# Layer 1's feed-forward blocks in the seven-product form, and the token sums on GpSimd

## The chip, the core and the metric

The kernel runs on one core of a Trainium2 chip. Five engines work side by side, each through its own instructions in order: TensorE (PE, matrix products), VectorE (DVE), ScalarE (ACT), GpSimd (POOL, which also issues the indirect DMAs) and SyncE (SP, which issues plain DMAs). They wait for one another through semaphores. The metric is the device time of one execution in microseconds (us); lower is better.

## The reference

Two layers of a graph transformer over 2708 tokens of width 512, f32, eight heads, each token attending to itself and its neighbours in `adj` (five to a few dozen):

```python
q = (h @ Wq.T + bq); k = (h @ Wk.T + bk); v = (h @ Wv.T + bv)
scores = einsum('nhd,mhd->hnm', q, k) / sqrt(64)     # -1e9 where mask == 0
ctx = einsum('hnm,mhd->nhd', softmax(scores), v)
h1 = layer_norm(h + ctx @ Wo.T + bo)
ff = relu(h1 @ W1.T + b1) @ W2.T + b2                # W1: 2048 x 512
h2 = layer_norm(h1 + ff)
```

## The kernel before

The kernel (`by_edges`) sorts the tokens by their number of neighbours into 22 tiles of 128 (the last has 20) and works on eleven **blocks** of two tiles. The order of all five engines is written out by hand: what stands first in the code stands first in its engine's queue.

The attention runs on DVE, ACT and POOL alone. For each tile, POOL gathers the rows of keys and values of its neighbours (L1113, one gather for one neighbour of 128 tokens; two gathers make a **chunk**). DVE multiplies keys by q (L1150), sums over a head's 64 columns (L1156), ACT makes the exponentials and scales half of the values (L1169, L1176), DVE scales the other half (L1182) and adds up (L1189). `advance(x)` in the block loop puts about x chunks of this into the queues; the tables `PACE` and `PACE7` say how much at which f. `until(g)` puts all that tile g still needs.

PE does the dense work. One block's feed-forward is a loop over 16 slices f of the 2048 hidden columns: four products of 256 columns into `pf` (L1523, or L1653 in the other form), ACT's relu into `ft`, and then the second product with W2. In the **plain form** (`feed_forward`) this is one 512-column product for each f and tile, into `a0` and `a1` (L1496). In the **seven-product form** (`feed_forward_by_seven`) two slices f and the two halves of W2's columns are taken together as a 2 x 2 product of 128 x 128 and 128 x 256 parts, and by sums of the parts (Strassen's, in Winograd's form) seven 256-column products replace eight. It needs for each of the seven pairs j four **token sums** of 128 x 128 (`sums`, L1625 to L1628, on DVE), three **weight sums** t2, t3, t4 and one changed quarter of W2 (`form`, L1592 to L1595), and at the block's end eight adds out of four PSUM places (a0, a1, c0, c1; L1695 to L1703) instead of two (L1567). The eighth pair is done plainly. The sums of pair j-1 are issued at f = 2j, the products of pair j-2 after the odd f (`products`). The three slots for t2, t3, t4 are reloaded from DRAM for every pair (`ask_forms`, L1610).

Layer 0 has the plain form in blocks 0, 1 and 10 and the seven-product form in blocks 2 to 9; the weight sums are made in block 1. All of layer 1 has the plain form. In layer 0, each block also has the K and V products of the block before (`keys_values`, L1732 to L1740). In the middle of each block the next block's o product is made (L620 from `attended`), added to the residual (L1455) and normalised; the norm's reciprocal root is one POOL instruction (L1275), between two DVE instructions (L1276, L1281). At a layer-1 block's end the two tiles zA and zB are normalised and scattered to the output by POOL (L1076). The queries of layer 1 are made before its first block, except those of tiles 21 and 0, which are made in block 0 (`asking`).

Of the kernel before, what the change touches and what calls it, by code (L numbers as in the profile page):

```python
# [483 lines left out]
def by_edges(ctx: ExitStack, tc: tile.TileContext, x, xT, adj, layers, out, redo):  # L484
# [71 lines left out]
    form_d = dram.tile([NFC // 2 - 1, 3, P, 2 * P], F32, name="form_d")  # L556
# [745 lines left out]
    class Layer:  # L1302
# [284 lines left out]
        def form(self, j):  # L1587
# [3 lines left out]
            t2, t3, t4 = self.slots if j < NFC // 2 - 2 else self.other_slots  # L1591
# [4 lines left out]
            for i, t in enumerate((t2, t3, t4)):  # L1596
                nc.sync.dma_start(out=form_d[j, i], in_=t)
# [7 lines left out]
        def ask_forms(self, upto):  # L1605

            while self.asked < upto:
                n = self.asked
                j, i = n // 3 % (NFC // 2 - 1), (2, 0, 1)[n % 3]
                nc.sync.dma_start(out=self.slots[i], in_=form_d[j, i])  # L1610
                self.asked += 1

        def feed_forward_by_seven(self, k, block, hs, hT):
# [6 lines left out]
            base = 3 * J * (k - FORMED - 1)  # L1620

            def sums(j):
                f0, f1 = fts[2 * j], fts[2 * j + 1]
                s = self.sums[j % 2]
                nc.vector.tensor_tensor(s[:, 0], f1[:, P:], f0[:, P:], ALU.add)  # L1625
                nc.vector.tensor_tensor(f0[:, P:], f0[:, :P], f0[:, P:], ALU.subtract)
                nc.vector.tensor_tensor(s[:, 1], s[:, 0], f0[:, :P], ALU.subtract)
                nc.vector.tensor_tensor(s[:, 2], f1[:, :P], s[:, 1], ALU.subtract)  # L1628
# [251 lines left out]
    for n in range(NL):  # L1880
        last = n == NL - 1
        nxt = None if last else Layer(n + 1, layers[n + 1])
        if n > 0:
# [37 lines left out]
            asking = now.queries(blocks[AHEAD])  # L1921
            next(asking)
            finish(streamed)
            now.apart = False
            now.load_w2(NFC // 2 - 1)
        hs, hT = early[n]
        projecting = xbs = None
        for k, block in enumerate(blocks):
            more = k + 1 < NB
            if k or n == 0:  # L1930
                asking = iter(())
            if n > 0 and 0 < k < NB - AHEAD:
                asking = now.queries(blocks[k + AHEAD])
# [9 lines left out]
            for f, zs in enumerate(working):  # L1943
# [16 lines left out]
                if more and f == NFC - 1:  # L1960
                    finish(asking)
# [120 lines left out]
```

## Time and profile before

| | us |
|---|---|
| median of three runs (1830.05 to 1832.14) | 1830.28 |
| span of the profiled execution | 1827.1 |
| layer 0, blocks 2 to 9, each | about 76.3 |
| layer 1, blocks 1 to 8, each | about 63.7 |

The profiled execution's own time is its span; the runs' times lie about 3 us above it. In the profile a row of a group names the line, the engine, the operation, what it writes and reads, the count, then the busy time, the mean of one in ns, and the idle time of the engine before it with what ended it. A row in order of time starts with the start and the length in us.

### The profile page before, as it was taken

What the parts mean: (1) busy time and instruction counts of PE and PEld (TensorE: products, weight loads), DVE (VectorE), ACT (ScalarE), POOL (GpSimd) and SP (SyncE); (2) the same over time, 40 slices, a digit from 0 to 9 for tenths busy, and PEclk for the clock granted to TensorE, in tenths of its full rate; (3) what the DMA queues carried; (4) which work ended last, traced back from release to release, by engine and by line L of the source; (5) the groups of instructions that cost most, each with busy time, mean ns of one, the idle gap of its engine ahead of it and who ended that gap; (6) DMA issues with size and microseconds to landing.
All of it is one profiled execution on the core that took longest, in us unless ns stands there. A gap on an engine that the chain in (4) does not pass through costs nothing.

```text
span 1827.1 us, 22528 instructions
## 1 busy us (share of the span) xinstructions
PE 1807.5 (99%) x6563; PEld 1162.6 (64%) x6563; DVE 1457.5 (80%) x2447; ACT 949.1 (52%) x3271; POOL 798.9 (44%) x745
## 2 busy tenths in 40 slices
PE   9999999999999999999999999999999999999998
PEld 4444456666777867778677644666666666666666
DVE  5887778988989889898895257887898888889853
ACT  5771435645556545564543213665665565567531
POOL 3334755534455544454430042353464555456302
PEclk9999999999999999999999999999999999999999
DMA  9997987757576676765652876745564664555300
GB/s 340 369 335 256 371 283 245 236 169 241 195 255 228 197 236 196 219 233 181 228 191 70 287 257 248 285 160 180 178 228 150 228 224 169 195 197 194 133 14 21
DMA packets 158061, 393.80 MB, mean 216 GB/s; under 512 B 17514, under 2 KB 60894, under 8 KB 157928
## 3 DMA queue, kind: packets, MB, share of 16 engines
q0 software_dynamic: 70608, 252.12, 40.2%
q1 hardware_dynamic: 77162, 118.55, 18.7%
q10 hardware_dynamic: 10158, 21.61, 3.1%
q8 instruction: 53, 0.87, 0.2%
q14 instruction: 80, 0.66, 0.1%
HBM read 338.78 MB, written 53.44 MB: 215 GB/s over the span
## 4 chain that ended last, share of the span: by engine, by line
PE 89%; DVE 5%; issue 2%; ACT 2%; DMA 1%; POOL 1%; POOLq 0%; SPq 0%; DVEq 0%
PE pf L1523 18%; PE a L1496 17%; PE pf L1653 9%; PE k L620 8%; PE v L620 8%; PE q L620 8%; PE o L620 8%; PE c L1643 4%; PE a L1643 3%; PE tp L1293 2%; DVE sc L1156 1%; DVE kv L1150 1%; DMA forms<-form_d 1%; PE a L1677 1%; PE a L1673 1%
## 5 line engine op out<-in xcount | busy, mean ns | idle before, releaser
L1113 POOL DMA_INDIRECT kv<-kv_d,listed x420 | 524.0, 1248 | 291.2 <-DVE acc L1189 133.9
L1523 PE MATMUL pf<-hT,w 128*128 128x256 f32 (+1 forms) x1792 | 393.2, 367 | 0.1
L1523 PEld LDWEIGHTS pf<-hT,w 128*128 128x128 f32 x1792 | 323.5, 190 | 103.1 <-issue 64.4
L1496 PE MATMUL a<-w,ft 128*128 128x512 f32 x800 | 373.1, 592 | 0.0
L1176 ACT ACTIVATE kv<-kv,p 128x64 f32<-128x64 f32 x1232 | 311.0, 335 | 5.0
L1275 POOL TENSOR_TENSOR rd<-va,mhalf 128x1 f32<-128x1 f32 (+1 forms) x88 | 80.5, 914 | 520.6 <-DVE va L1273 520.5
L1150 DVE TENSOR_TENSOR kv<-kv,q 128x1024 f32<-128x1024 f32 (+1 forms) x222 | 256.9, 1157 | 13.3 <-DMA q<-q_d,ident_i 10.9
L1156 DVE TENSOR_REDUCE sc<-kv 128x16 f32<-128x1024 f32 (+1 forms) x222 | 257.9, 1162 | 7.6
L1189 DVE TENSOR_TENSOR acc<-acc,kv 128x1024 f32<-128x1024 f32 (+2 forms) x178 | 205.4, 1154 | 37.6 <-ACT kv L1176 23.0
L1653 PE MATMUL pf<-hT,w 128*128 128x256 f32 x1024 | 233.1, 379 | 1.6 <-ACT ft L1664 1.6
L1496 PEld LDWEIGHTS a<-w,ft 128*128 128x128 f32 x800 | 150.1, 190 | 113.2 <-issue 101.3
L1653 PEld LDWEIGHTS pf<-hT,w 128*128 128x128 f32 x1024 | 193.9, 190 | 35.4 <-issue 7.9
L1534 ACT ACTIVATE ft<-pf,b 128x256 f32<-128x256 f32 (+1 forms) x208 | 95.0, 459 | 197.6 <-PE pf L1523 195.2
L1169 ACT ACTIVATE p<-sc,listed 128x8 f32<-128x8 f32 x420 | 104.0, 296 | 147.2 <-DVE sc L1156 135.7
L620 PE MATMUL o<-wo,cT 128*128 128x512 f32 x336 | 151.0, 593 | 1.0 <-ACT cT L1298 1.0
L1664 ACT ACTIVATE ft<-pf,b 128x256 f32<-128x256 f32 x96 | 44.9, 468 | 160.5 <-PE pf L1653 160.5
L1182 DVE TENSOR_TENSOR kv<-kv,p 128x512 f32<-128x512 f32 (+1 forms) x178 | 123.4, 693 | 4.5 <-ACT p L1169 4.3
L620 PEld LDWEIGHTS o<-wo,cT 128*128 128x128 f32 x336 | 63.4, 190 | 74.7 <-issue 65.5
L745 DVE MAX8 tops<-code 128x8 f32<-128x247 f32 (+2 forms) x242 | 78.6, 400 | 28.3 <-ACT code L740 28.3
L1281 DVE SCALAR_TENSOR_TENSOR h<-h,rd,ln_b 128x512 f32<-128x512 f32 (+1 forms) x88 | 65.9, 749 | 39.5 <-POOL rd L1275 39.5
L1220 ACT ACTIVATE cx<-acc,su 128x64 f32<-128x64 f32 (+1 forms) x352 | 88.2, 333 | 12.9 <-DVE su L1212 7.4
L1455 DVE TENSOR_TENSOR h<-o,xb 128x512 f32<-128x512 f32 (+1 forms) x44 | 30.3, 688 | 80.0 <-PE o L620 65.0
(232 smaller groups left out, 2323.5 us busy)
## 6 DMA issues: line engine op xcount, KB each, us to landing
aj<-in_adj SPq DMA_DIRECT2D x42, 677.0 KB, 6.3
forms<-form_d SPq DMA_DIRECT2D x168, 128.0 KB, 4.2
kv_d<-kvs ACTq DMA_DIRECT2D x21, 512.0 KB, 5.5
xg<-in_xT SPq DMA_DIRECT2D x19, 512.0 KB, 7.4
w<-in_W SPq DMA_DIRECT2D x16, 512.0 KB, 6.2
kv<-kv_d,listed POOLq DMA_INDIRECT x420, 6.3
zT_d<-zT SPq DMA_DIRECT2D x22, 256.0 KB, 5.1
xb_d<-h SPq DMA_DIRECT2D x21, 256.0 KB, 5.7
```

The source lines that it names most:

```text
L620: nc.tensor.matmul(o[:r], xs(c), wm[:, c, :], start=(c == 0), stop=(c == NC - 1))
L1113: return nc.gpsimd.indirect_dma_start(out=to, out_offset=None, in_=table[:, :], in_offset=bass.IndirectOffsetOnAxis(ap=s, axis=0), bounds_ ...
L1150: nc.vector.tensor_tensor(kv[:r, :c, :DM], kv[:r, :c, :DM], self.q[:r].unsqueeze(1).to_broadcast([r, c, DM]), ALU.mult,)
L1156: nc.vector.tensor_reduce(self.sc[:r, s0 : s0 + c, :], kv[:r, :c, :DM].rearrange("p s (h d) -> p s h d", d=DK), AX.X, ALU.add,)
L1169: nc.scalar.activation(p[:r, s, :], self.sc[:r, s, :], AF.Exp, bias=minus[:r, g, s : s + 1])
L1176: nc.scalar.activation(to[:, i, hd], kv[:r, i, DM + h * DK : DM + (h + 1) * DK], AF.Copy, scale=p[:r, s0 + i, h : h + 1],)
L1182: nc.vector.tensor_tensor(to[:, 0, :].rearrange("p (h d) -> p h d", d=DK), kv[:r, 0, DM:].rearrange("p (h d) -> p h d", d=DK), p[:r, s0, : ...
L1189: nc.vector.tensor_tensor(self.acc[:r, :c, :], self.acc[:r, :c, :], kv[:r, :c, DM:], ALU.add)
L1496: nc.tensor.matmul(a[:r, cols], fts[f][:, c0 : c0 + r], self.w2[f // 2][:, f % 2, cols], start=(f == 0), stop=(f == NFC - 1),)
L1523: nc.tensor.matmul(pf[:, :w], self.w1[f // 2][:, c, f % 2 * P : f % 2 * P + P], hT[:, c, :w], start=(c == 0), stop=(c == NC - 1),)
L1643: nc.tensor.matmul(to, left, right, start=start, stop=stop)
L1653: nc.tensor.matmul(pf[:, :W], self.w1[j][:, c, f % 2 * P : f % 2 * P + P], hT[:, c, :], start=(c == 0), stop=(c == NC - 1),)
```

## The change

Layer 1's blocks 0 to 9 take the seven-product form (`FIRST7`), with a pace table of their own. The weight sums of layer 1 are made in layer 0's last block, at f = 7, 9, ... 15 and after the first two queries, into places of the gathers' buffers (`staged`), and stored to a DRAM tile for each layer. All queries of layer 1 come before its first block, so that the place of Wq is free for the slots. The four token sums go from DVE to POOL, in both layers. The pools of `pf` and of the other products have two PSUM places each in layer 1, as in layer 0's blocks of that form, instead of three. The scatters of zA and zB stand behind each tile's norm.

```diff
-PACE7 = (0.0,) * 4 + (0.6,) + (1.3,) * 4 + (0.6,) * 2 + (0.0,) * 2 + (0.5, 0.8, 2.4)
+PACE7 = (
+    (0.0,) * 4 + (0.6,) + (1.3,) * 4 + (0.6,) * 2 + (0.0,) * 2 + (0.5, 0.8, 2.4),
+    (0.0,) * 3 + (0.7, 0.7, 1.2, 0.7, 1.2, 0.7, 1.2, 0.6, 0.0, 0.0, 1.0, 0.7, 1.9),
+)
 FORMED = 1
+FIRST7 = (FORMED + 1, 0)
...
-    form_d = dram.tile([NFC // 2 - 1, 3, P, 2 * P], F32, name="form_d")
+    form_d = [dram.tile([NFC // 2 - 1, 3, P, 2 * P], F32, name=f"form_d{n}") for n in range(NL)]
...
-        def form(self, j):
+        def staged(self):
+            slots = []
+            for _ in range(3):
+                place = at.tile([P, SLOTS, 2 * DM], F32, tag="kv", name="forms", bufs=KVB)
+                place = place.rearrange("p s n -> p (s n)")
+                slots += [place[:, i * 2 * P : (i + 1) * 2 * P] for i in range(8)]
+            return [slots[3 * j : 3 * j + 3] for j in range(NFC // 2 - 1)]
+
+        def form(self, j, slots=None):
...
-            t2, t3, t4 = self.slots if j < NFC // 2 - 2 else self.other_slots
+            t2, t3, t4 = slots or (self.slots if j < NFC // 2 - 2 else self.other_slots)
...
-                nc.vector.tensor_tensor(s[:, 0], f1[:, P:], f0[:, P:], ALU.add)
-                nc.vector.tensor_tensor(f0[:, P:], f0[:, :P], f0[:, P:], ALU.subtract)
-                nc.vector.tensor_tensor(s[:, 1], s[:, 0], f0[:, :P], ALU.subtract)
-                nc.vector.tensor_tensor(s[:, 2], f1[:, :P], s[:, 1], ALU.subtract)
+                nc.gpsimd.tensor_tensor(s[:, 0], f1[:, P:], f0[:, P:], ALU.add)
+                nc.gpsimd.tensor_tensor(f0[:, P:], f0[:, :P], f0[:, P:], ALU.subtract)
+                nc.gpsimd.tensor_tensor(s[:, 1], s[:, 0], f0[:, :P], ALU.subtract)
+                nc.gpsimd.tensor_tensor(s[:, 2], f1[:, :P], s[:, 1], ALU.subtract)
...
             norm(zA, P, self.g2, self.e2, between=lambda: stB.append(spread(zB)))
+            if self.n == NL - 1:
+                put(out, ident_i[:, block[0] : block[0] + 1], zA, "out")
             norm(zB, P, self.g2, self.e2, stB[0])
+            if self.n == NL - 1:
+                put(out, ident_i[:, block[1] : block[1] + 1], zB, "out")
...
-            streamed = now.queries(order[18 : 2 * AHEAD])
+            streamed = now.queries(order[18:])
             next(streamed)
             now.query(order[17], both[:, 1])
-            advance(0.6)
-            next(streamed)
-            advance(0.6)
+            for _ in order[18:21]:
+                advance(0.6)
+                next(streamed)
...
             now.load_w2(NFC // 2 - 1)
+            now.prepared()
...
-            seven = n == 0 and FORMED < k < NB - 1
+            seven = FIRST7[n] <= k < NB - 1
...
-            if n == 0 and k in (FORMED + 1, NB - 1):
+            if k in (FIRST7[n], NB - 1):
                 places_of_psum(3 - seven, seven)
...
                         nxt.load_second(0, temp)
+                        staged = nxt.staged()
+                    if f > 6 and f % 2:
+                        nxt.form((f - 7) // 2, staged[(f - 7) // 2])
...
                 nxt.query(*pool.pop(0))
+                nxt.form(6 - len(pool) % 2, staged[6 - len(pool) % 2])
```

The line numbers of the new program differ by 4 to 17. POOL's queue in a layer-1 block before, from one block's end to the next o (rd is the reciprocal root, out the scatter to the output, kv a gather):

```order
L1275 TENSOR_TENSOR rd<-va,mhalf 128x1
L1076 DMA out<-h,ident_i 2708x512
L1275 TENSOR_TENSOR rd<-va,mhalf 128x1
L1076 DMA out<-h,ident_i 2708x512
L1113 DMA kv<-kv_d_112,listed 128x1024 x14
L1275 TENSOR_TENSOR rd<-va,mhalf 128x1 x2
```

The same place in the new program, up to the third of the block's seven groups of token sums (`forms` and `ft` are the places of the sums and of the relu's results):

```order
L1279 TENSOR_TENSOR rd<-va,mhalf 128x1
L1080 DMA out<-h,ident_i 2708x512
L1279 TENSOR_TENSOR rd<-va,mhalf 128x1
L1080 DMA out<-h,ident_i 2708x512
L1638 TENSOR_TENSOR forms<-ft 128x128
L1639 TENSOR_TENSOR ft<-ft 128x128
L1640 TENSOR_TENSOR forms<-forms,ft 128x128
L1641 TENSOR_TENSOR forms<-ft,forms 128x128
L1117 DMA kv<-kv_d_112,listed 128x1024 x2
...
L1117 DMA kv<-kv_d_112,listed 128x1024 x4
L1638 TENSOR_TENSOR forms<-forms 128x128
```

Five groups of four sums now stand between the second scatter and the root of the next o, among the gathers; a sixth stands between the two roots and a seventh behind them.

DVE's queue at the end of a layer-1 block before (h is first the block's input with the residual, then the output; a is PSUM):

```order
L1567 TENSOR_TENSOR h<-a_10928,h 128x512
L1269 BN_STATS st<-h 128x6
L1271 BN_AGGR mv<-st 128x2
L1273 TENSOR_SCALAR va<-mv 128x1
L1276 SCALAR_TENSOR_TENSOR h<-h,mv,ln_g 128x512
L1281 SCALAR_TENSOR_TENSOR h<-h,rd,ln_b 128x512
L1150 TENSOR_TENSOR kv<-kv,q 128x2x512
```

The same place in the new program (u are the partial results of the two sums that both tiles share):

```order
L1193 TENSOR_TENSOR acc<-acc,kv 128x1024
L1709 TENSOR_TENSOR h<-u_10752,h 128x256
L1710 TENSOR_TENSOR u_10752<-c_10197,u_10752 128x256
L1711 TENSOR_TENSOR u_10753<-c_10198,u_10752 128x512
L1712 TENSOR_TENSOR h<-c_10198,h 128x256
L1713 TENSOR_TENSOR h<-a_10195,h 128x512
L1714 TENSOR_TENSOR h<-a_10196,h 128x512
L1715 TENSOR_TENSOR h<-u_10753,h 128x256
L1716 TENSOR_TENSOR h<-h,u_10753 128x512
L1273 BN_STATS st<-h 128x6
```

Eight adds stand where each tile had one, ahead of both norms.

More of the change, by code (lines that the diff above doesn't have):

```diff
@@ L1596, in form @@
             for i, t in enumerate((t2, t3, t4)):
-                nc.sync.dma_start(out=form_d[j, i], in_=t)
+                nc.sync.dma_start(out=form_d[self.n][j, i], in_=t)
         def form_back(self, j):
@@ L1609, in ask_forms @@
                 j, i = n // 3 % (NFC // 2 - 1), (2, 0, 1)[n % 3]
-                nc.sync.dma_start(out=self.slots[i], in_=form_d[j, i])
+                nc.sync.dma_start(out=self.slots[i], in_=form_d[self.n][j, i])
                 self.asked += 1
@@ L1619, in feed_forward_by_seven @@
             fts = []
[L1620 removed]
+            base = 3 * J * (k - FIRST7[self.n])
             def sums(j):
@@ L1929, in by_edges @@
             more = k + 1 < NB
[L1930 to L1933, printed above, removed]
-            seven = n == 0 and FORMED < k < NB - 1
+            seven = FIRST7[n] <= k < NB - 1
             if n == 0 and k == FORMED:
                 now.prepared()
-            if n == 0 and k in (FORMED + 1, NB - 1):
+            if k in (FIRST7[n], NB - 1):
                 places_of_psum(3 - seven, seven)
@@ L1960, in by_edges @@
                 if more and f == NFC - 1:
-                    finish(asking)
                     hT = now.turned(blocks[k + 1], hs_next)
-                advance((PACE7 if seven else (PACE if k else PACES)[n])[f])
-                if f in (0, 3, 7, 9) and (f or k):
-                    next(asking, None)
+                advance((PACE7[n] if seven else (PACE if k else PACES)[n])[f])
                 if k == 0 and len(now.w1) < NFC // 2 and f % 2 == 0:
```

2 lines of the change are left out of this document (removed).

## The prediction

> **What bounds the kernel now.** I read the page first, then the chain in order of time, then the windows block by block, then who waits for whom on VectorE (DVE) and GpSimd (POOL).
>
> ```profile
> span 1827.1 us, 22528 instructions
> PE 1807.5 (99%) x6563; PEld 1162.6 (64%) x6563; DVE 1457.5 (80%) x2447; ACT 949.1 (52%) x3271; POOL 798.9 (44%) x745
> ```
>
> TensorE (PE) has work in 99% of the span. That is the bound of the average; the change acts on one kind of stage, the layer-1 blocks, so I read the bound there.
>
> ```profile
> 1398.27 5.15 PE a L1496 x12
> 1403.42 6.91 PE pf L1523 x32
> ```
>
> A 512-column matmul instruction takes 5.15/12 = 0.429 us of PE, a 256-column one 6.91/32 = 0.216 us, back to back. Both forms run at the same rate per column.
>
> ```profile
> 1334.50:1398.30 63.80, 63.80 (x226) 41.21 (x225) 59.21 (x80) 37.67 (x142) 33.38 (x28) 1.00 0.59 212
> ...
> sum 382.30, PE 382.30 PEld 246.78 DVE 337.49 ACT 237.22 POOL 194.65; mean PE 63.72 PEld 41.13 DVE 56.25 ACT 39.54 POOL 32.44
> DVE h L1455 <- PE o L620: 22.3, 9, 3.6
> DVE h L1281 <- POOL rd L1275: 12.0, 24, 1.6
> ```
>
> The columns of a window are its length, then PE, weight loads, DVE, ACT, POOL, the granted clock and the DMA share. Six layer-1 blocks in a row take 63.7 us each; PE has no gap, DVE works 56.25 us of each. DVE's idle time is 382.3 - 337.5 = 44.8 us in six blocks. Of this, 22.3 us is waiting for PE's o product, 3.7 us a block. That is all the slack DVE has; the other 22.5 us (3.75 a block) are waits on POOL and ACT that stay. So PE bounds these blocks, with DVE 3.7 us behind it.
>
> **What PE gives up.** A pair of f has four 512-column products, eight instructions, 8 x 0.429 = 3.43 us; in the new form seven 256-column products, 14 x 0.216 = 3.02 us. That is 0.41 us a pair, 2.9 a block of seven pairs, 28.6 us over ten blocks: a PE floor of 63.7 - 2.9 = 60.8 us. It is real only where nothing else is later than 60.8.
>
> **What DVE gets.** The end of a layer-1 block has two adds now; in the new form it has the eight adds that layer 0's blocks already show.
>
> ```profile
> L1567 DVE TENSOR_TENSOR h<-a,h 128x512 f32<-128x512 f32 x12 | 7.9, 661 | 0.0
> 621.72 0.37 ACT L1695 COPY u<-c 128x256 f32<-128x256 f32 x1 [0.62 <-PE c L1643]
> 622.81 10.52 PE L1653 MATMUL pf<-hT,w 128*128 128x256 f32 x48
> 624.12 0.37 DVE L1696 TENSOR_TENSOR h<-u,h 128x256 f32<-128x256 f32 x1
> 628.20 0.68 DVE L1269 BATCH_NORM_STATS2 st<-h 128x6 f32<-128x512 f32 x1
> 631.62 0.93 POOL L1275 TENSOR_TENSOR rd<-va,mhalf 128x1 f32<-128x1 f32 x1 [1.25 <-DVE va L1273]
> 633.78 0.28 DVE L1627 TENSOR_TENSOR forms<-forms,ft 128x128 f32<-128x128 f32 x1
> 634.48 0.59 PE L1643 MATMUL c<-forms 128*128 128x256 f32 x2
> ```
>
> Eight adds take 628.20 - 624.12 = 4.1 us against 2 x 0.66 = 1.3: DVE 56.25 + 2.8 = 59.0 us. To the waits that stay (3.75) come two. First, on POOL the scatter of zA to the output stands between the two reciprocal roots of a block end, and the second root waits behind it. The block in which that happened already shows it:
>
> ```profile
> 1409.70 0.75 DVE L1281 SCALAR_TENSOR_TENSOR h<-h,rd,ln_b 128x512 f32<-128x512 f32 x1 [1.57 <-POOL rd L1275]
> 1443.50 0.69 DVE L1455 TENSOR_TENSOR h<-o,xb 128x512 f32<-128x512 f32 x1 [0.29 <-PE o L620]
> 1446.45 0.75 DVE L1281 SCALAR_TENSOR_TENSOR h<-h,rd,ln_b 128x512 f32<-128x512 f32 x1 [0.46 <-POOL rd L1275]
> 1450.82 0.69 DVE L1455 TENSOR_TENSOR h<-o,xb 128x512 f32<-128x512 f32 x1 [3.62 <-PE o L620]
> ```
>
> 1.57 us instead of 0.46: +1.1. Second, with two PSUM places instead of three the second o product (8 x 0.429 = 3.4 us) cannot start before DVE has emptied the first (0.69), while DVE's norm lasts from 1443.50 to 1447.20, 3.7: 4.1 - 3.7, some 0.5 us of the 3.62 remains however late DVE is. Need of DVE: 59.0 + 3.75 + 1.1 + 0.5 = 64.4 us a block. That is above the floor of 60.8 and 0.7 above today's 63.7. **DVE takes over as the bound** and eats the whole saving before the sums on POOL have cost anything.
>
> **What the sums on POOL cost.** In layer 1 they are new, 28 a block; in layer 0 they leave DVE. The trace has no f32 128x128 add on POOL; the nearest rows:
>
> ```profile
> L958 POOL TENSOR_TENSOR kvs<-kvs,bk 128x512 f32<-128x512 f32 x20 | 25.4, 1272 | 52.4 <-ACT kvs L956 43.3 <-issue 4.7 <-DMA aj<-in_adj 4.3
> L734 POOL TENSOR_TENSOR aj<-aj,diag 128x128 int32<-128x128 int32 x20 | 8.7, 433 | 29.6 <-DMA aj<-in_adj 29.6
> 148.07 0.17 DVE L803 TENSOR_TENSOR run<-run 128x22 f32<-128x22 f32 x1
> 148.28 1.29 POOL L958 TENSOR_TENSOR kvs<-kvs,bk 128x512 f32<-128x512 f32 x1 [2.43 <-issue]
> 148.36 1.25 DVE L803 TENSOR_TENSOR run<-run 128x20 f32<-128x20 f32 x1
> ```
>
> I take 0.43 us, the same shape in int32. The last three rows are the dearest finding: a DVE add of two SBUF inputs that takes 0.17 us alone took 1.25 beside a POOL add, and ended 0.04 us after it (149.61 against 149.57). It was held until about 0.13 us before POOL's end. The other way round, gathers show it:
>
> ```profile
> 1421.12 1.23 DVE L1189 TENSOR_TENSOR acc<-acc,kv 128x1024 f32<-128x1024 f32 x1
> 1421.56 1.65 POOL L1113 DMA_INDIRECT kv<-kv_d,listed  x1 [0.30 <-issue]
> 1422.26 1.22 DVE L1150 TENSOR_TENSOR kv<-kv,q 128x1024 f32<-128x1024 f32 x1
> 1423.51 0.99 POOL L1113 DMA_INDIRECT kv<-kv_d,listed  x1 [0.30 <-issue]
> ```
>
> A gather beside a one-input reduce takes 0.99; beside L1189 it took 0.66 more, and got in at that add's end although L1150 stood ready. So a sum waits for the end of the DVE instruction in front, and the next DVE instruction waits for the sum if it too has two SBUF inputs: 0.43 - 0.13 = 0.30 us. Bounds for a block: nothing, or 28 x 0.30 = 8.4 us. A burst of four that meets the one-input reduce passes for nothing, one that meets the three two-input instructions in a row pays twice or so. I take 10 of 28, **3.0 us**.
>
> The Trainium skill speaks against the change here ("SBUF — State Buffer", section "Who interferes with whom"): a DVE instruction with two SBUF inputs contends with a GpSimd instruction that reads SBUF, because GpSimd's one read port is DVE's second, and whichever comes second is blocked until the first is done. By that wording a hold lasts the whole 0.43 us, 10 holds make 4.3 us a block, and the total would be about 10 us longer than mine; the row above ends the hold 0.13 us earlier, and I go by the row.
>
> **What stands in POOL's queue.** POOL is in order, and DVE's norm after the first o waits for a root that stands behind five bursts and some 14 gathers.
>
> ```profile
> L1113 POOL DMA_INDIRECT kv<-kv_d,listed x127 | 156.7, 1234 | 38.0 <-issue 27.6 <-DVE sc L1156 2.7 <-ACT ft L1534 1.8
> L1076 POOL DMA_INDIRECT out<-h,ident_i x12 | 17.4, 1449 | 14.5 <-DVE h L1281 11.9 <-DVE va L1273 2.6
> 1445.48 0.93 POOL L1275 TENSOR_TENSOR rd<-va,mhalf 128x1 f32<-128x1 f32 x1 [8.74 <-DVE va L1273]
> ```
>
> POOL has 8.7 us to spare there, a little more once DVE is slower. Five bursts need 5 x 4 x 0.43 = 8.6 us unblocked; blocked at 3 to 3.5 us a burst, 15 to 17. Bounds 0 and 6 us of DVE waiting a block; most of a late burst runs unblocked once DVE stands still, so I take 1.0. Block: 64.4 + 3.0 + 1.0 = **68.4, +4.7**. PE meanwhile waits twice: at the first products (in the layer-0 rows above DVE's third sum ends at 634.06 and PE needs it at 634.48, 11.7 us after the block's start; in layer 1 both scatters come first), and at the second o.
>
> **Blocks with less DVE work.**
>
> ```profile
> 1143.00:1206.00 63.00, 63.00 (x228) 40.14 (x227) 51.58 (x68) 35.86 (x135) 25.52 (x23) 1.00 0.63 228
> 1716.80:1778.40 61.60, 61.60 (x226) 39.32 (x225) 39.97 (x56) 27.99 (x104) 9.81 (x9) 1.00 0.15 51
> sum 457.50, PE 454.45 PEld 340.58 DVE 405.88 ACT 253.38 POOL 223.29; mean PE 75.74 PEld 56.76 DVE 67.65 ACT 42.23 POOL 37.22
> L1626 DVE TENSOR_TENSOR ft<-ft 128x128 f32<-128x128 f32 x40 | 11.9, 297 | 1.4
> L1595 DVE TENSOR_TENSOR forms<-w,forms 128x256 f32<-128x256 f32 x7 | 3.0, 425 | 0.2
> forms<-form_d SPq DMA_DIRECT2D x168, 128.0 KB, 4.2
> ```
>
> Layer 1's first and tenth blocks (rows one and two) leave DVE idle for 11 and 22 us, so PE stays the bound. They gain 2.9 and lose the wait at the first products: in the layer-0 rows the second root ends 7.3 us after block start (632.55 - 622.81, less the 2.4 by which DVE came late); the first scatter adds 1.3, the last step of the norm 0.75, the second scatter 0.3 and 1.45, three sums 1.3: 12.4 against the 10.8 at which PE needs them (48 x 0.216 + 0.43). 2 x (1.6 - 2.9) = **-2**. Layer 0's eight seven-form blocks (row three: six of them, 76.25 us, PE 75.74) can gain at most 0.5 each. DVE loses 28 x 0.29 = 8.1 us of work, gets about 3 back in holds, and is no bound; but the first sums now start behind the last step of the norm, up to 1.3 us later than PE needs them. Bounds -4 and +10 in all; I take **+2**, since DVE's lateness of 2.4 us shrinks with its load. Weight sums in layer 0's last block: 28 x 0.42 = 12 us on DVE, which is half idle there; two of the seven stand between the queries and the K adds that PE waits for, 3.4 us at worst: **+2**. The 21 stores follow them on SP, where the loads of W1 and W2 wait behind; these loads wait for PE anyway. The 210 form loads of layer 1 take 4.2 us each in the median; a slot is free 5.9 us before its next use (seven products 3.0 + two f 3.4, less one product): nothing where DVE bounds. Layer 1's last two queries only move ahead of block one: nothing.
>
> Layer 1's other eight blocks give 8 x 4.7 = +37.6. Sum 37.6 - 2 + 2 + 2 = +39.6: a span of 1866.7 us. The median run of before, 1830.28, is 3.2 above the profiled span; **1870 us**.
>
> **Rivals.** (1) *PE stays the bound, faster.* If sums slip into DVE's one-input gaps at no price and the 3.75 us of waits shrink once DVE runs behind (they are waits on ACT and POOL, which then are ahead), DVE needs 59.0 + 2.5 to 3, about 62 us. It decides at 63.7: below that, eight blocks gain 1.7 each, the other two 1.3, layer 0 up to 4: about 1811 us. For it: one block today gets by with 59.2 us of DVE work and 4.6 idle. Against it: the held add of 1.25 us. (2) *DVE bounds, but holds cost almost nothing*, 64.4 less the 0.5 or so that lateness hides: eight blocks at about 63.7, so 1828 to 1834, no change. Late form loads belong here: they would take from a gain and not add to a loss. (3) *POOL becomes the bound*: bursts of 3.5 us, the full 6 us at the root and 4 of holds, 74 us a block, 8 x 10.7 = +86: about 1918. For it: 21 gathers of 1.23 + 0.30 (32 us), four roots and two scatters (7) and 7 x 3.5 of sums make 63 us in order, before any wait. Against it: a standing DVE clears the port. (4) *The change does not do what it says* (PE's products not replaced): excluded by the new order; the saving is made and lost again.
>
> **How the numbers follow.** Forecast, DVE bound with moderate holds, 1845 to 1895: 0.52. POOL as the bound, above that: 0.12; of it about half lies over 1902. Small holds, 1834 to 1845: 0.08. No change within 0.2% (1826.6 to 1833.9, about what a measurement of this kernel can tell from none): 0.12. Faster: 0.16. So faster 0.16, same 0.12, slower 0.72. The range 1822 to 1902 leaves out most of rival 1 (0.13) and half of rival 3 (0.06).
>
> **What would show it.** Right: layer-1 blocks of 66 to 70 us with PE idle before the first c product (waiting for POOL's sums) and before the second o, and DVE without its wait for o at the first one; two-input DVE instructions (L1150, L1189) whose means are up by 0.1 us or more while the one-input reduce does not change; POOL sums of 0.4 us alone and over 1 us beside DVE. Wrong: blocks near 61 us with PE busy throughout; DVE means unchanged; DVE still waiting 3 us for o in each block. In layer 0, blocks off 76.3 by over 1.5 us would refute the +2.

## The result, and the profile after

| kernel | median us (range, runs) | against before, 95% interval |
|---|---|---|
| before | 1831.2 (1830.1 to 1832.9, 4) | |
| changed | 1927.8 (1923.2 to 1930.4, 4) | 1.0529 [1.0515, 1.0543] |

The change costs 5.3%. The direction was as forecast; the size was not: 1927.8 lies above the forecast of 1870 and above the range's end of 1902. First the head, the chain and two groups of the page of the changed kernel (a group's row: line, engine, operation, count, busy time, mean in ns, then the idle time before it and what ended it):

```profile
span 1928.6 us, 24655 instructions
PE 1813.8 (94%) x7023; PEld 1263.4 (66%) x7023; DVE 1471.9 (76%) x2311; ACT 952.0 (49%) x3281; POOL 1134.8 (59%) x1249
PE 57%; DVE 15%; POOL 9%; issue 9%; ACT 4%; DMA 4%; SPq 0%; POOLq 0%; DVEq 0%; ACTq 0%
L1154 DVE TENSOR_TENSOR kv<-kv,q 128x1024 f32<-128x1024 f32 (+1 forms) x222 | 270.2, 1217 | 44.7 <-DMA kv<-kv_d,listed 32.3
L1656 PE MATMUL c<-forms 128*128 128x256 f32 x324 | 99.5, 407 | 75.6 <-POOL forms L1640 72.1
```

TensorE fell from 99% to 94% of the span. Two waits stand out that the page of before did not have: TensorE for the third sum on GpSimd (72.1 us), and VectorE for gathered rows (32.3 us). GpSimd's busy time rose from 798.9 to 1134.8. No engine is full; so the question is which of them the others follow.

Where the 101.5 us of span came from, by the time at which a block's first add stands on VectorE: layer 0 13; layer 1's queries and first block 9; its eight blocks with a full load 75.7; the tenth block 6; the end -2. The eight blocks, block ends 1211.2 to 1722.2 before and 1233.1 to 1819.8 after, as one window each (length, then PE, weight loads, DVE, ACT, POOL, granted clock, DMA share):

```profile
1211.20:1722.20 511.00, 509.95 (x1793) 328.91 (x1793) 446.42 (x592) 314.30 (x1181) 257.36 (x213) 1.00 0.54 191
```

```profile
1233.10:1819.80 586.70, 512.69 (x2161) 410.24 (x2161) 485.85 (x641) 318.76 (x1199) 416.01 (x438) 0.94 0.62 206
```

63.9 us a block became 73.3: +9.4, where +4.7 was forecast. Now VectorE's waits in these two windows (us in total, times, longest), before and after:

```profile
DVE h L1455 <- PE o L620: 35.1, 13, 4.3
DVE h L1281 <- POOL rd L1275: 15.7, 32, 1.6
```

```profile
DVE kv L1154 <- DMA kv<-kv_d,listed: 29.9, 17, 4.7
DVE h L1285 <- POOL rd L1279: 25.5, 24, 2.8
DVE h L1459 <- PE o L624: 15.8, 6, 4.9
DVE acc L1193 <- ACT kv L1180: 9.5, 7, 1.6
DVE kv L1186 <- ACT p L1173: 5.3, 3, 3.6
```

VectorE's time can be summed: 39.4 us more busy; waits for gathers 29.9, for roots +9.8, for ACT 14.8, for o -19.3. That makes 74.6 of the 75.7. Such a sum always closes for one engine; it does not say that this engine sets the time. TensorE's sum closes too, by its wait for the sums. One block's start shows both (start and length in us, engine, line, what; in brackets the idle time before it and what ended it):

```profile
1393.36 0.59 PE L1656 MATMUL a<-forms,ft 128*128 128x256 f32 x2
1404.13 1.22 PE L1656 MATMUL c<-forms 128*128 128x256 f32 x2 [10.17 <-POOL forms L1640]
```

```profile
1399.34 1.23 POOL L1080 DMA_INDIRECT out<-h,ident_i  x1 [1.08 <-DVE h L1285]
1400.60 0.68 POOL L1638 TENSOR_TENSOR forms<-ft 128x128 f32<-128x128 f32 x1
1401.36 1.32 POOL L1639 TENSOR_TENSOR ft<-ft 128x128 f32<-128x128 f32 x1
1402.64 1.43 POOL L1640 TENSOR_TENSOR forms<-forms,ft 128x128 f32<-128x128 f32 x1
1404.15 0.46 POOL L1641 TENSOR_TENSOR forms<-ft,forms 128x128 f32<-128x128 f32 x1
...
1408.33 1.05 POOL L1117 DMA_INDIRECT kv<-kv_d,listed  x1 [0.15 <-issue]
```

```profile
1402.29 1.47 DVE L1154 TENSOR_TENSOR kv<-kv,q 128x1024 f32<-128x1024 f32 x1
...
1410.68 0.20 DVE L1216 RECIPROCAL su<-su 128x8 f32<-128x8 f32 x1
1415.60 1.23 DVE L1154 TENSOR_TENSOR kv<-kv,q 128x1024 f32<-128x1024 f32 x1 [4.72 <-DMA kv<-kv_d,listed]
```

GpSimd starts its first sums only behind the block end's second scatter, and the third of them takes 1.43 us beside a busy VectorE. TensorE stands for 10.2 us. In this block two groups of sums go ahead of the first gather, which starts at 1408.33, and VectorE then stands for 4.7 us with nothing to multiply. (So it is in three of the eight blocks; in the other five, two gathers come between the first group and the second.) VectorE's multiplication at 1402.29 takes 1.47 us instead of 1.22.

### The profile page after: what moved, and what is told of

Its sections match the earlier page's. It is cut to its first block, busy times and chain, and to the rows that moved or that the text cites. A ratio compares the mean times of both kernels' runs of the same rounds, so it can differ in the third digit from the quotient of the medians.

```text
span 1928.6 us, 24655 instructions
## 1 busy us (share of the span) xinstructions
PE 1813.8 (94%) x7023; PEld 1263.4 (66%) x7023; DVE 1471.9 (76%) x2311; ACT 952.0 (49%) x3281; POOL 1134.8 (59%) x1249
## 4 chain that ended last, share of the span: by engine, by line
PE 57%; DVE 15%; POOL 9%; issue 9%; ACT 4%; DMA 4%; SPq 0%; POOLq 0%; DVEq 0%; ACTq 0%
PE pf L1666 11%; PE k L624 8%; PE v L624 7%; PE c L1656 7%; PE o L624 6%; PE q L624 6%; PE a L1656 5%; DVE kv L1154 3%; DVE sc L1160 3%; PE pf L1527 3%; POOL kv L1117 2%; ACT kv L1180 2%; PE a L1500 2%; DMA forms<-form_d 2%; POOL forms L1640 2%
## 5 line engine op out<-in xcount | busy, mean ns | idle before, releaser
L1117 POOL DMA_INDIRECT kv<-kv_d,listed x420 | 509.5, 1213 | 190.1 <-issue 107.5
L1666 PE MATMUL pf<-hT,w 128*128 128x256 f32 x2304 | 523.0, 379 | 4.6 <-issue 2.1
L1154 DVE TENSOR_TENSOR kv<-kv,q 128x1024 f32<-128x1024 f32 (+1 forms) x222 | 270.2, 1217 | 44.7 <-DMA kv<-kv_d,listed 32.3
L1677 ACT ACTIVATE ft<-pf,b 128x256 f32<-128x256 f32 x216 | 101.0, 469 | 363.1 <-PE pf L1666 338.3
L1193 DVE TENSOR_TENSOR acc<-acc,kv 128x1024 f32<-128x1024 f32 (+2 forms) x178 | 210.9, 1185 | 60.7 <-ACT kv L1180 45.4
L1656 PE MATMUL c<-forms 128*128 128x256 f32 x324 | 99.5, 407 | 75.6 <-POOL forms L1640 72.1
L1656 PEld LDWEIGHTS c<-forms 128*128 128x128 f32 x324 | 60.9, 197 | 94.4 <-POOL forms L1640 79.8
L1656 PE MATMUL c<-w,forms 128*128 128x256 f32 x324 | 99.7, 390 | 0.0
L1656 PE MATMUL a<-w,forms 128*128 128x256 f32 x324 | 97.6, 383 | 0.0
L1527 PE MATMUL pf<-hT,w 128*128 128x256 f32 (+1 forms) x512 | 95.6, 336 | 1.5 <-ACT cx L1224 0.9
```

The source lines that it names most:

```text
L1117: return nc.gpsimd.indirect_dma_start(out=to, out_offset=None, in_=table[:, :], in_offset=bass.IndirectOffsetOnAxis(ap=s, axis=0), bounds_ ...
L1154: nc.vector.tensor_tensor(kv[:r, :c, :DM], kv[:r, :c, :DM], self.q[:r].unsqueeze(1).to_broadcast([r, c, DM]), ALU.mult,)
L1193: nc.vector.tensor_tensor(self.acc[:r, :c, :], self.acc[:r, :c, :], kv[:r, :c, DM:], ALU.add)
L1527: nc.tensor.matmul(pf[:, :w], self.w1[f // 2][:, c, f % 2 * P : f % 2 * P + P], hT[:, c, :w], start=(c == 0), stop=(c == NC - 1),)
L1656: nc.tensor.matmul(to, left, right, start=start, stop=stop)
L1666: nc.tensor.matmul(pf[:, :W], self.w1[j][:, c, f % 2 * P : f % 2 * P + P], hT[:, c, :], start=(c == 0), stop=(c == NC - 1),)
```

## The experiments

Two theories stood at the beginning. **A** is the prediction's: VectorE's path sets a layer-1 block; without any sums it needs 64.4 us, and holds at the port and GpSimd's queue come on top. **B**: TensorE sets it, by its wait for the first sums. All runs, in the order of this section:

| run | median us (range) | against before, 95% interval |
|---|---|---|
| sums left out in layer 1 | 1877.5 (1875.8 to 1878.1) | 1.0265 [1.0248, 1.0282] |
| sums made, not read | 1920.2 (1918.2 to 1923.5) | 1.0498 [1.0481, 1.0516] |
| no sums, six adds fewer | 1852.7 (1850.0 to 1856.1) | 1.0137 [1.0120, 1.0154] |
| no sums, second o earlier | 1869.2 (1867.4 to 1871.3) | 1.0217 [1.0200, 1.0234] |
| no sums, pf in pairs | 1922.1 (1918.2 to 1923.3) | 1.0506 [1.0488, 1.0523] |
| sums not read, and later | 1897.0 (1895.1 to 1899.7) | 1.0372 [1.0354, 1.0389] |
| adds on an own buffer | 1894.6 (1890.1 to 1895.5) | 1.0347 [1.0328, 1.0367] |
| memsets in their place | 1881.5 (1877.3 to 1882.8) | 1.0286 [1.0269, 1.0304] |
| first sums on VectorE | 1903.0 (1898.2 to 1906.6) | 1.0399 [1.0379, 1.0419] |
| all layer-1 sums on VectorE | 1929.3 (1927.2 to 1931.2) | 1.0540 [1.0522, 1.0558] |
| scatters later | 1914.1 (1913.3 to 1915.6) | 1.0462 [1.0445, 1.0480] |
| only layer 0's sums on GpSimd | 1835.1 (1832.6 to 1836.0) | 1.0032 [1.0020, 1.0045] |
| more attention in the queries | 1921.2 (1918.4 to 1923.9) | 1.0510 [1.0493, 1.0528] |
| five edits together | 1902.5 (1897.6 to 1907.6) | 1.0399 [1.0370, 1.0427] |
| three parts together | 1891.9 (1890.3 to 1895.1) | 1.0351 [1.0334, 1.0369] |

### Is it TensorE's wait for the sums?

In the first run the sums of layer 1 are not made; in the second they are made and nobody reads them.

```diff
+                s0, s1, s2, fd = s[:, 0], s[:, 1], s[:, 2], f0[:, P:]
+                if self.n == 1:
+                    s0 = s1 = s2 = fd = f1[:, P:]
...
-                if f % 2 == 0 and j > 0:
+                if f % 2 == 0 and j > 0 and self.n == 0:
                     sums(j - 1)
```

(The last lines are in the first run only.)

> Layer 1's token sums are left out and its products read parts of the relu's results in their place (that part of the computation is left out; layer 0 keeps its sums on GpSimd). Theory A (as predicted): VectorE bounds the eight full blocks of layer 1 with 64.4 us before any cost of the sums, so eight blocks go from 73.3 us (mean after the change) to 64.4: 1927.8 - 71 = about 1855. Theory B: TensorE bounds them, and only the wait for the first sums made them long, so they fall to TensorE's floor of 60.8 plus about 1: 1927.8 - 8 x 11.5 - 6 (block nine) = about 1830. In both the wait of TensorE before the first c product goes away.

> Layer 1's sums are made on GpSimd as in the changed kernel, but its products read parts of the relu's results instead (the output of the feed-forward in layer 1 is left out). GpSimd's queue, the port and VectorE's load stay as they are; only TensorE no longer waits for a sum. Theory A (as predicted): held VectorE instructions and the queue before the root of the o norm made the blocks long, so they stay: 1905 to 1930. Theory B: the wait of TensorE for the first sums (9 us a block, and about 2 us of half clock behind it) made them long: ten blocks lose 8 to 11 us each, 1927.8 - 95 = about 1835, at most 1850. What the time has above that of the kernel without sums is the price of holds and queue alone.

Measured 1877.5 and 1920.2. With unread sums the eight blocks take as long as with read ones, and TensorE waits elsewhere. The run with unread sums, window of the eight blocks and TensorE's first two waits in it:

```profile
1230.80:1818.70 587.90, 525.61 (x2176) 416.21 (x2176) 486.30 (x641) 319.36 (x1201) 409.92 (x438) 0.94 0.62 205
PE pf L1669 <- ACT ft L1680: 48.5, 18, 6.2
PE o L624 <- ACT cT L1302: 12.9, 6, 3.1
```

587.9 against 586.7. The 61 us that TensorE spent waiting for sums became 48.5 us before pf, where it waits for ACT's relu, which is queued behind exponentials of VectorE's scores. **B falls for these blocks**: TensorE's wait was slack. B holds in the tenth block, where VectorE has little work: 64.7 us with read sums, 58.8 with unread ones, most of the 7.6 us between the two medians.

But A was not right either: without any sums the eight blocks take 68.1 us, not 64.4.

```profile
1229.60:1774.50 544.90, 502.94 (x2156) 400.11 (x2155) 469.54 (x641) 317.84 (x1199) 255.69 (x214) 0.98 0.64 221
DVE h L1459 <- PE o L624: 31.7, 10, 4.9
DVE h L1285 <- POOL rd L1279: 19.7, 24, 1.6
DVE acc L1193 <- ACT kv L1180: 7.4, 6, 1.5
```

VectorE is busy 58.7 us a block, as forecast (59.0). Its wait for o is 31.7 us, 4.0 a block, where 0.5 was forecast: it hardly shrank from the 35.1 of before, although VectorE got later.

### Why 68.1 without any sums?

```diff
-            nc.vector.tensor_tensor(zA[:, L], u2, zA[:, L], ALU.add)
+            if self.n == 0:
+                nc.vector.tensor_tensor(zA[:, L], u2, zA[:, L], ALU.add)
```

(and so for the other five adds that read c0, c1 or what was made of them)

> Layer 1's token sums are left out as in the first run (1877.5 us), and at the end of its blocks also the six adds out of c0, c1 and their sums (only the adds of a0 and a1 to the two tiles stay): 2.8 us less of VectorE's work a block. If VectorE's path bounds these blocks: 8 to 9 blocks x 2.8 = 24 less, about 1853. If TensorE and VectorE wait for each other at the o products whatever VectorE's load is: under 8 less, 1870 to 1878.

1852.7: 24.8 less, the full price of the adds. The window of its eight blocks:

```profile
1227.60:1746.10 518.50, 498.06 (x2160) 397.66 (x2159) 448.12 (x593) 317.57 (x1199) 256.10 (x214) 0.99 0.66 232
DVE h L1459 <- PE o L624: 27.1, 10, 4.9
```

64.8 us a block, 3.3 less for 2.7 us less of VectorE's work, so **VectorE's path bounds**. TensorE's waits for the relu before pf fell along, from 25.9 to 2.5 us, though nothing on TensorE or ACT was edited: they follow VectorE. More than that: VectorE's load is now that of before (56.0 against 55.8 us a block), TensorE is busy for 1.5 us a block less than before (62.3 against 63.7), and the block is still not shorter than the 63.9 of before. VectorE's waits for roots are 0.5 us a block longer than before (19.8 us in the eight blocks against 15.7); its waits for ACT, of which the eight blocks of before show none, are 9.7 us; its wait for o is only 8.0 us shorter (27.1 against 35.1), although VectorE's path now bounds. So, as an estimate from these rows, some 1 us a block of its waiting for o was slack before the change and not 3.7: most of it was part of its path. The new pace table and the two PSUM places, which also differ from the kernel before, were not put back by themselves.

The timeline of the run without sums shows why these waits do not go away (TensorE, ACT, then VectorE):

```profile
1471.37 5.40 PE L624 MATMUL o<-wo,cT 128*128 128x512 f32 x8 [2.28 <-ACT cT L1302]
...
1480.06 1.89 PE L1669 MATMUL pf<-hT,w 128*128 128x256 f32 x8
1481.79 3.60 PE L624 MATMUL o<-wo,cT 128*128 128x512 f32 x8
```

```profile
1468.16 0.49 ACT L1173 ACTIVATE p<-sc,listed 128x8 f32<-128x8 f32 x2 [1.42 <-DVE sc L1160]
...
1470.96 1.11 ACT L1302 ACTIVATE cT<-tp,bv 128x128 f32<-128x128 f32 x4
```

```profile
1473.14 1.22 DVE L1193 TENSOR_TENSOR acc<-acc,kv 128x1024 f32<-128x1024 f32 x1
1476.81 0.69 DVE L1459 TENSOR_TENSOR h<-o,xb 128x512 f32<-128x512 f32 x1 [2.44 <-PE o L624]
1485.43 0.69 DVE L1459 TENSOR_TENSOR h<-o,xb 128x512 f32<-128x512 f32 x1 [4.93 <-PE o L624]
```

The first o needs cT, ACT's copy of the first tile's transposed context, and that copy stands in ACT's queue behind exponentials of the second tile's scores, for which ACT waits on VectorE. So a later VectorE makes the first o later too. Between the two o products TensorE has four transposes, seven products, a pf and the o itself, 8.6 us; VectorE's norm takes 3.7. Where VectorE stood ready at the first o, as here and in two more of the eight blocks, the difference, 4.9, is left as a wait; in the other five VectorE still had attention to do when the first o was there, and it waited 0 to 4.7 us for the second. In the eight blocks together the waits for the second o are 25.0 us, as before the change (24.7), and those for the first 6.7 (before, 10.4).

Two edits of that place. In the first, `products(3)` moves behind the second o; in this form the relu of f = 12 takes the place of that of f = 6 before these products, which so read other data. In the second, two slices share one PSUM place.

```diff
-                if f % 2 and j > 1:
+                if f % 2 and j > 1 and not (self.n == 1 and f == 11):
                     products(j - 2)
+                if self.n == 1 and f == 12:
+                    products(3)
```

```diff
-                pf = ps_f.tile([P, DM], F32, tag="f", name="pf")
+                if f % 2 == 0 or self.n == 0:
+                    both_pf = ps_f.tile([P, DM], F32, tag="f", name="pf")
+                pf = both_pf[:, f % 2 * W :] if self.n == 1 else both_pf
```

> Layer 1's token sums are left out as in the first run (its eight full blocks took 68.1 us there), and in layer 1 the seven products of pair 3 are issued on TensorE behind the second o product instead of ahead of it. Theory C1: VectorE's path is the bound, and it holds a wait for the second o (4.9 us in a block looked at) because 3.0 us of products, 1.7 of pf and 3.4 of the o product itself follow the first o on TensorE. Then 2 to 3 us a block go: 1877.5 - 20 = about 1857. Theory C2: TensorE's waits for the relu behind two PSUM places are the loss: no change, 1873 to 1882.

> Layer 1's token sums are left out as in the first run, and in layer 1 the two slices of a pair take the two halves of one PSUM place of pf, so that TensorE can run four slices ahead of the relu instead of two. Theory C2: TensorE's 27.6 us of waiting for the relu (ACT, in order behind the exponentials of a late VectorE) are the loss: 1877.5 - 25 = about 1852. Theory C1: they are slack of an engine that isn't the bound: no change, 1872 to 1882.

The first gave 8.3 us, less than half of what C1 expected and more than C2 allows. VectorE's waits in its eight blocks:

```profile
DVE acc L1193 <- ACT kv L1180: 18.0, 15, 1.6
DVE h L1459 <- PE o L624: 10.1, 6, 2.4
```

The wait for o went from 31.7 to 10.1 as C1 says, but its waits for ACT rose in the same trace, from 7.4 to 18.0 for scaled values and from 1.4 to 5.5 for exponentials, and of the 21.6 us only 7.0 came off the eight blocks (537.9 against 544.9). So the order on TensorE is a part of the 68.1; what else goes round in this chain from VectorE over ACT and TensorE back to VectorE was not taken apart. The second run missed both expectations: 45 us slower. TensorE's waits for the relu before pf rose from 25.9 to 42.2 us (15 to 40 times): with two slices in one place TensorE seems to wait for both relus of the place before it may write one half. That reading was not tested further, and neither were four places of their own; so this run does not decide on C2. The waits for the relu that fell in the run with six adds fewer speak against it.

### What the sums cost: queue and holds

```diff
-                if f % 2 == 0 and j > 0:
-                    sums(j - 1)
+                if f % 2 == 0 and j > self.n:
+                    sums(j - 1 - self.n)
```

> As the run with unread sums (GpSimd makes layer 1's token sums, the products there read parts of the relu's results: the output of its feed-forward is left out), with each group of sums issued two slices f later, so that the first two groups stand behind gathers instead of ahead of all of them. Theory Q (the queue): VectorE's waits for gathered rows, 3 to 5 us a block, come from the first two groups ahead of the gathers, and go: 1920 - 25 = about 1895. Theory H (holds at the port): the same 28 sums hold VectorE the same wherever they stand: 1915 to 1925.

1897.0: 23 us less, as Q expects. VectorE's waits for gathers went from 30.8 us (unread sums in the old place) to 7.9:

```profile
DVE kv L1154 <- DMA kv<-kv_d,listed: 7.9, 6, 2.4
```

The remaining 19.5 us above the run without sums are the subject of the next two.

```diff
+            def dummies(j):
+                s = self.sums[j % 2]
+                for i in range(4):
+                    nc.gpsimd.tensor_tensor(s[:, i % 2], s[:, 2], s[:, 2], ALU.add)
```

(in the other run `nc.gpsimd.memset(s, 0.0)`)

> Layer 1's token sums are left out as in the first run (1877.5 us); in their place, two slices f later, GpSimd makes four adds of 128x128 for each pair that touch only a buffer of their own, so that nobody waits for their data and they wait for none. Theory H (holds): they hold VectorE's two-input instructions as the sums do, 2 us a block: mean of L1154 about 1.28 us for 1024 columns against 1.214, time 1892 to 1900. Theory R: what the later sums still cost (19.5 us) came from the relu, which waits on ACT until GpSimd has read its place: then 1877 to 1885 and the holds cost nothing.

> As the run with adds on a buffer of their own, but each add is a GpSimd memset of 128x384, which reads no SBUF. If VectorE is held by GpSimd's reads alone: L1154 back at 1.214 us and 1876 to 1884. If any GpSimd access to SBUF holds it: L1154 as long as beside the adds, in proportion to the memset's own length, and a time up by as much.

1894.6 and 1881.5. The groups of GpSimd's instruction and of VectorE's multiplication in the eight blocks, with adds, then with memsets:

```profile
L1648 POOL TENSOR_TENSOR forms<-forms 128x128 f32<-128x128 f32 x224 | 127.0, 595 | 1.0
L1154 DVE TENSOR_TENSOR kv<-kv,q 128x1024 f32<-128x1024 f32 x78 | 99.5, 1276 | 7.1 <-DMA kv<-kv_d,listed 6.6 <-issue 0.5
```

```profile
L1154 DVE TENSOR_TENSOR kv<-kv,q 128x1024 f32<-128x1024 f32 x78 | 94.8, 1215 | 5.0 <-DMA kv<-kv_d,listed 4.3 <-issue 0.6
L1648 POOL MEMSET forms<- 128x384 f32 x224 | 94.3, 421 | 9.7
```

Adds that no one waits for cost 17 us, nearly what the later sums do, so theory R falls. 224 memsets of 0.42 us leave L1154 at 1.215 us, its time without sums (1.214); the adds bring it to 1.276, the changed kernel's 1.278. The hold comes from GpSimd's reading. The Trainium skill ("SBUF — State Buffer", section "Who interferes with whom") says that a VectorE instruction with two SBUF inputs contends with a GpSimd instruction that reads SBUF and not with one that only writes it; the runs agree. The hold was short: the held L1154 shown above took 0.25 us more, where a sum that nothing disturbs takes 0.46 in all.

### Which engine for the sums

```diff
+                engine = nc.vector if self.n == 1 and j == 0 else nc.gpsimd
-                nc.gpsimd.tensor_tensor(s[:, 0], f1[:, P:], f0[:, P:], ALU.add)
+                engine.tensor_tensor(s[:, 0], f1[:, P:], f0[:, P:], ALU.add)
```

(and so for the other three; in the second run without `and j == 0`)

> In layer 1 the four sums of the first pair of each block go back to VectorE; the other six groups stay on GpSimd. Theory A (VectorE bounds): 4 x 0.29 = 1.2 us more of VectorE's work a block less some holds: 1928 to 1938. Theory B (TensorE waits for the first sums): they no longer stand behind the second scatter (1.7 us with its gap) nor in a burst of 3.5 us up to the third sum, but 0.9 us behind the norm's last step, so TensorE's wait falls from about 9 to about 5 us a block: nine to ten blocks x 4.3 = about 40 less, 1885 to 1895.

> The changed kernel with all of layer 1's token sums back on VectorE (layer 0's stay on GpSimd). If VectorE's path is the bound and its waits for o stay: 68.1 (without sums) + 8.1 = 76.2 us a block against 73.3: 1927.8 + 23 = about 1950. If the 3.9 us a block by which it waits for o shrink as it gets later: 72.3, about 1920. If TensorE's wait for the first sums on GpSimd were the loss: well below 1900.

First sums back: 1903.0, 24.8 less, between the two expectations and inside neither. All back: 1929.3, the same as all on GpSimd; VectorE's waits for o shrank from 31.7 us without sums to 21.4, in part as the second expectation has it. So layer 1's sums cost VectorE's path as much on GpSimd as on VectorE itself; the four that stood ahead of the gathers cost more there than they save. With the first sums on VectorE its waits for gathers in the eight blocks almost vanish (29.9 us in the changed kernel):

```profile
DVE kv L1154 <- DMA kv<-kv_d,listed: 2.4, 3, 1.5
```

TensorE's wait shrinks as well, which B expected; by the run with unread sums that can count in the tenth block alone, which went from 64.7 to 60.2.

### The smaller terms

```diff
             norm(zB, P, self.g2, self.e2, stB[0])
-            if self.n == NL - 1:
-                put(out, ident_i[:, block[1] : block[1] + 1], zB, "out")
...
+                if f == 4:
+                    while unput:
+                        g, z = unput.pop(0)
+                        put(out, ident_i[:, g : g + 1], z, "out")
```

> The changed kernel with layer 1's two scatters of a block issued at f = 4 of the next block, behind the second group of sums. By the prediction's term: VectorE's wait for the second root at a block's end falls from 1.57 to 0.46 us, 1.1 x 10 = 11 less: about 1917; the first sums also come 2.5 us earlier, which matters only where TensorE is the bound (block nine, 3 us). If the gathers behind them matter (they move behind the same two scatters as before): no more than that. No effect would be 1923 to 1932.

> The kernel before with one edit: the token sums of layer 0's eight seven-product blocks on GpSimd. By the prediction's term: +2 us on 1831.2, about 1833. By the changed kernel's trace, in which these blocks take 0.95 us more each: +7.6, about 1839. If the sums in layer 0 cost by themselves nothing, 1831.

> The changed kernel with 1.2 instead of 0.6 chunks of attention at three places of layer 1's last queries. If the 9 us by which layer 1's queries and first block grew are attention that VectorE makes too late for the first o: the 10.7 us of TensorE's waiting there shrink by 4 to 8: 1920 to 1924. If VectorE waits for the queries anyway: no change, 1925 to 1931.

The scatters' place costs 13.7 us, near the 11 expected; VectorE's waits for roots in the eight blocks fell from 25.5 to 17.4. Layer 0's sums on GpSimd cost 6.8 us by themselves, not 2; TensorE's waits for them in blocks 1 to 9 show most of it, and it had no such waits before:

```profile
PE c L1643 <- POOL forms L1627: 3.8, 7, 0.6
PE c L1643 <- POOL forms L1625: 1.0, 2, 0.5
```

The run with more attention among layer 1's queries came out at 1921.2, inside the first expectation, but it is inconclusive: in its profiled execution layer 0, which has the same code, already ended 6.0 us earlier than in the changed kernel's, and the stretch of queries and first block was longer (174.1 against 168.2 us) with later blocks shorter. Why that stretch grew by 9 us stays open. It did so in the run without sums too (168.8), so it is not the sums.

### Together

> A try to get the best of the parts: the changed kernel with layer 0's sums and the first two groups of each layer-1 block back on VectorE, the second o product ahead of the products of pair 3, the scatters at f = 4 of the next block, and 1.2 instead of 0.6 chunks at three places of layer 1's last queries. Sum of the parts as measured or expected: -25 (first sums), -7 (layer 0), -8 (o), -10 (scatters), -5 (queries): 1927.8 - 55 = about 1873, still slower than before. If the parts overlap, 1880 to 1895; if VectorE is relieved enough for TensorE to bound, below 1850.

> The changed kernel with the sums of layer 0 and of the first pair of each layer-1 block on VectorE, and layer 1's scatters at f = 4 of the next block. If the parts add up: 1903.0 (first sums) - 7 (layer 0) - 13.7 (scatters) = about 1882. If the scatters overlap with the first sums: up to 1893.

The five edits together gave 1902.5, no better than the first sums alone. As in the run above, the products of pair 3 read what f = 12 wrote; and the second group, 1.2 us a block, is back on VectorE. The three parts that keep the computation gave 1891.9, where the sum of the parts was 1882. VectorE's waits for roots stayed low there (16.3 us in the eight blocks), but its waits for gathers, 2.4 with the first sums back alone, were 13.2: the scatters now stand among the gathers, which may be why; that is argued, not shown. It is the best form of the change found here, and 3.5% slower than the kernel before. None of the runs beats that kernel.

## Why the prediction was right in direction and wrong in size

The terms of a layer-1 block with full load, in us, forecast and measured (eight-block windows, divided by eight; VectorE's adds and the first figure for o from the runs without sums):

| term | forecast | measured |
|---|---|---|
| VectorE's adds at the block's end | +2.8 | +2.7, for 3.3 of time |
| wait for o | -3.2 (3.7 to 0.5) | -0.4 without sums; -2.4 in the changed kernel |
| roots, by scatter and queue | +1.1 and +1.0 | +1.2 |
| holds | +3.0 | +2.0 (485.85 - 469.54 busy) |
| gathers late | not in the sum | +3.7 |
| waits for ACT | unchanged | +1.9 |
| block | +4.7 | +9.4 |

- **"DVE takes over as the bound"**: right, shown for the kernel without sums by the run with six adds fewer. So was the finding that the saving on TensorE is lost before the sums cost anything.
- **The step that failed first** is "That is all the slack DVE has", and after it "some 0.5 us of the 3.62 remains however late DVE is". A wait that VectorE had for TensorE was read as slack. Most of it was made by the order on TensorE behind a first o product that itself follows VectorE's scores. The prediction gave that order only the second o's own 3.4 us; the seven products and the pf ahead of it were left out. In the run without sums VectorE waited 4.0 us a block for o, 3.1 of it for the second, instead of 0.5. A block without sums lay 3.7 us above the forecast (68.1 for 64.4), and 3.5 of that is this wait; the block with sums lay 4.9 above (73.3 for 68.4). With the products moved, waits for ACT took most of the wait's place: that it stays is shown, what makes it is shown in part.
- **The second** is the place of GpSimd's queue. It was priced at the root of the o norm (1.0 of 6 us), and there it cost little. The price fell on the gathers behind the first sums: VectorE waited 3.7 us a block for gathered rows, 0.3 with the first group alone back on VectorE, and the run that moved the groups was 23 us shorter. The order shown ahead of the prediction had the first group ahead of the gathers in plain sight.
- **Holds**: the mechanism was right and the size 2.0 instead of 3.0.
- **Blocks with less VectorE work**: the sum "12.4 against the 10.8" gave TensorE 1.6 us of waiting. In the tenth block it waited 7.3 us. The sum left out that VectorE comes late to the block's end and that the three sums took 0.5 to 1.4 us beside it, not 0.43 each.
- **Layer 0**: +2 was forecast, 6.8 measured alone, inside the bounds of -4 to +10. The reason given (the first sums behind the norm) fits the waits above. Layer 0's last block, with the weight sums, took 52.8 us instead of 48.6: +4, not +2.
- **Outside the eight blocks** the forecast had +2 in all, and some 26 was measured (13 + 9 + 6 - 2). The 9 of layer 1's queries and first block stay open.
- **Rival 3**, POOL as the bound with 74 us a block, came nearest in time (1918), but not in its mechanism: GpSimd is busy 416 of 586.7 us there, and still waits for VectorE.

## What to carry to other kernels

A wait of engine X for engine Y is slack only if Y would have been there had X come later; look at what Y's own sequence waits for before counting it. Work that is moved to an in-order queue costs at what stands behind it, so look at every transfer behind the new place, and move the work there piece by piece: here four of 28 sums a block made half of the 50 us that all of them cost. The cheapest test of such a chain is to keep the moved work and let nobody read it.

## What the hardware showed

GpSimd instructions that only write did not slow VectorE (above). And TensorE's granted clock fell to half after short gaps, though not after each. The run without sums, a row of TensorE with the gap before it, then three windows of 3.4 us (the seventh number, instruction counts left out, is the granted clock):

```profile
1460.18 1.99 PE L1669 MATMUL pf<-hT,w 128*128 128x256 f32 x8 [3.32 <-ACT ft L1680]
```

```profile
1458.30:1461.70 3.40, 1.51 (x7) 1.36 (x8) 3.30 (x4) 3.37 (x15) 2.79 (x3) 1.00 1.00 390
1468.50:1471.90 3.40, 1.12 (x4) 0.49 (x3) 3.26 (x4) 3.37 (x14) 0.00 (x0) 1.00 1.04 403
1471.90:1475.30 3.40, 3.40 (x6) 1.33 (x5) 2.36 (x3) 0.54 (x2) 0.00 (x0) 0.51 0.57 224
```

The first window holds the end of the gap of 3.32 us; TensorE worked 1.51 us in it, and the clock was 1.00 in the 3.4 us behind it too. The second holds the gap of 2.28 us ahead of the o product; TensorE worked 1.12 us in it, the clock was halved in the next, and the o product there took 5.40 us instead of 3.60, on VectorE's path. The Trainium skill ("TensorE: Matmul & The Clock Gate", section "HAM oscillation — how this bites in real kernels") warns of idle gaps of more than about 3.4 us. Here a gap of 2.28 us was enough, and one of 3.32 was not: the length of the gap alone did not decide here; what does was not tested. In the changed kernel the same halving follows each of the nine waits for sums in the eight blocks (granted clock 0.94 over these blocks), but as TensorE does not bound there, it should cost little, except on an o product that VectorE waits for; that is argued, not shown. It was not tried to keep the clock up with idle products.
